# An adaLN transformer block on one core: batch one reordered, x reloaded into eight tiles, the last batch's norms moved by DMA

## The chip, the cores and the metric

The kernel runs on one core of one Trainium2 chip. The metric is the device time of one execution in microseconds (us). Engines are named as the profile names them: PE is TensorE (PEld its weight loads), DVE is VectorE, ACT is ScalarE, POOL is GpSimd, SP is SyncE. A name with a q behind it (SPq, ACTq, POOLq) is an engine's instruction queue, mostly where it issues DMAs.

## The reference

Four batches of 1024 tokens with 512 channels, all in float32. Six rows of modulation per batch come from a small vector c. Then an attention step and a linear FFN step, each with its layer norm, its shift and scale, and its gate:

```python
mod = (silu(c) @ wmod).reshape(B, 6, 1, 512)        # sa, ca, ga, sb, cb, gb
ga, gb = sign(ga) * max(|ga|, 0.25), sign(gb) * max(|gb|, 0.25)
h = layernorm(x) * (1 + ca) + sa
q, k = h @ Wq.T, h @ Wk.T                           # rank 64; every head has the same scores
attn = softmax(16 heads alike: sum over r of q_ir * k_jr)
x = x + ga * ((attn @ (h @ Wv.T)) @ Wo.T)
h = layernorm(x) * (1 + cb) + sb
x = x + gb * (sum over r of h @ factors[r] / sqrt(8) + bias)
```

## The kernel before

All 16 heads share one score matrix, so the attention is one 1024 x 1024 product per batch. Tokens are cut into eight tiles of 128 and two halves of four tiles. The matrices Wv and Wo are multiplied once into wvo, the eight factors are summed once into fsum, and the shift of the first norm goes through wvo into one row c1 per batch, which is added to x.

For each batch b the work is:

- ln1: statistics and normalized tiles xn (L309, L318), turned into hT. For batch zero PE transposes them (L331); for the others DVE transposes 32 x 32 blocks (L382) and 16 small DMAs, move_blocks (L371), put the blocks in place. A block is 64 KB. All of them are issued on SP unless another queue is named.
- project (L414), then scores for four pairs of token tiles (L460), each with a row maximum on DVE (nm, L476), an exponential on ACT (L480) and a transpose: by PE for pairs 0 and 1 of batch zero (L501), by DVE and move_blocks otherwise (L489, L371). Score tiles have two PSUM buffers, probability tiles two in SBUF.
- z: probabilities times xn for the two halves of query tokens. Batch zero does it plainly (z_steps, L527, two parts for each of four channel chunks); later batches use seven products of half size in place of eight (z_steps_by_seven, L595, steps m1, m5, m2, m6, m7, m3, m4), with sums on DVE and POOL around them.
- attn_out (o0 to o7, L665): z times w, where w is wvo scaled by ca and ga (make_w, L645); DVE adds the result into x (L670) and takes statistics. add_c1 (L362) adds the c1 row to x, bc_c being that row spread over all partitions by a DMA from DRAM.
- ln2: normalized tiles (L318) to hT_f. For batches zero to two DVE transposes blocks (L695), move_blocks brings them to a tile st (L371) and ACT applies shift and scale (L701). For the last batch PE transposes them (ln2_transposes, L331), woven between products. add_bias (L710) adds the bias row.
- ffn (f0 to f7, L725): hT_f times f, where f is fsum times the gate (make_f, L658); DVE adds x (L730) and a DMA stores the tile (L733).

PSUM products share four banks (ps_m). Batches are staggered: while batch b does its second half of z and attn_out, the projections and scores of batch b + 1 run between the steps; the FFN of batch b runs inside the first half of z of batch b + 1. The order is written out in the code, and a framework then places each engine's instructions and its waits. Each engine works its list in order.

The x tiles have twelve buffers: eight in use and four for the next batch (load_x, L101). For batches after the first, load_x goes to POOL's queue, as do the stores, so a load into a tile whose store is under way waits on that queue. xa tiles are a second read of x for ln1 of the next batch (load_xa, L112). The tiles st have one buffer; the spread rows (bc) have two. The factors are loaded and summed on POOL in batch zero (L285 to L293).

At the start the weights wv and wo come in four pieces each beside the x tiles of batch zero, all on SP. mod_products (L179) multiplies silu(c) with the modulation weights; for the rows sa and ca (name a) only two of the four column groups of PE are used, for the other four rows (name b) all four. mod_rows copies the PSUM rows to SBUF (L188), channels turns them by tiny PE transposes (L196), and qbias (L239) follows. shift_product (L251) makes c1 from sa and wvo.

Of the kernel before, what the change touches and what calls it, by code (L numbers as in the profile page):

```python
# [30 lines left out]
def kernel(  # L31
# [39 lines left out]
    stp = ctx.enter_context(tc.tile_pool(name="stp", bufs=1))  # L71
# [9 lines left out]
    def psum_mm(name):  # L81
        return ps_m.tile([P, 512], F32, tag="mm", name=name)
# [9 lines left out]
    nc.sync.dma_start(out=cTs, in_=cT.rearrange("(kc p) b -> p kc b", p=P))  # L92
# [5 lines left out]
    def load_x(b, t):  # L98
        tl = xp.tile([P, D], F32, tag="x", bufs=NT + GT, name=f"x_{b}_{t}")
        queue = nc.sync if b == 0 else nc.gpsimd  # L100
        queue.dma_start(out=tl, in_=x[b, ts(t, P), :])  # L101
        xt[b, t] = tl
        if b == 0:
            xa[b, t] = tl
# [16 lines left out]
    for cc in range(KC):  # L121
        nc.sync.dma_start(out=wvs[:, cc, :], in_=wv[ts(cc, P), :])
        nc.sync.dma_start(out=wos[:, cc, :], in_=woT[ts(cc, P), :])
        for t in range(2 * cc, 2 * cc + 2):
            load_x(0, t)
# [30 lines left out]
    scT = const.tile([P, KC, B], F32, name="scT")  # L156
    nc.vector.reciprocal(scT, en)
    nc.vector.tensor_tensor(scT, cTs, scT, ALU.mult)
# [26 lines left out]
    def mod_rows(ps, count, dst):  # L185
        rows = []
        for g in range(count):
            nc.vector.tensor_copy(dst[:, g, :], ps[32 * g : 32 * g + B, :])  # L188
            rows.append(dst[:, g, :])
        return rows  # L190
# [41 lines left out]
    def first_rows():  # L232
        sa_r, ca_r = mod_rows(mod_products([0, 1], "a"), 2, rows_a)
        first["sa"] = channels(sa_r, 0, "sa", 0.0)
        first["ca1"] = channels(ca_r, 0, "ca", 1.0)

        ps = psum_mm("ps_qbias")
        for kc in range(KC):
            nc.tensor.matmul(  # L239
                ps[: 2 * R, :B], wqk[:, kc, :], first["sa"][:, kc, :],  # L240
                start=(kc == 0), stop=(kc == KC - 1),
            )
        nc.vector.tensor_copy(qbias, ps[: 2 * R, :B])
# [3 lines left out]
    def shift_product():  # L247

        ps = psum_mm("ps_c1")
        for kc in range(KC):  # L250
            nc.tensor.matmul(  # L251
                ps[:B, :], first["sa"][:, kc, :], wvo[:, kc, :],
                start=(kc == 0), stop=(kc == KC - 1),
            )
        nc.vector.tensor_copy(rows_a[:, 2, :], ps[:B, :])
# [103 lines left out]
    def add_c1(b):  # L359
        bc = spread("c1", b)  # L360
        for t in range(NT):
            nc.vector.tensor_tensor(xt[b, t], xt[b, t], bc, ALU.add)  # L362

    def move_blocks(src, dst, queue=nc.sync):

        for r in range(NQ):
            for c in range(NQ):  # L370
                queue.dma_start(out=dst[ts(c, Q), r], in_=src[ts(r, Q), c])  # L371
# [307 lines left out]
    def ln2(b, g):  # L679


        if g == 0:
            bias_b[b] = spread("gbias", b)
        hT = hT2[b, g] = hp.tile([P, KC, GW], F32, tag="hT", name=f"hT_f_{b}_{g}")
        if b + 1 == B:
            xn = prp.tile([P, GT, D], F32, tag="pr", name=f"xn_f_{b}_{g}")
            xn2[b, g] = normalize(b, halves(g), mv2[b], xn, f"f_{b}_{g}")
        else:

            xn = hT.rearrange("p k w -> p (k w)")  # L690
            normalize(
                b, halves(g), mv2[b],
                xn.rearrange("p (c k t a) -> p t k c a", c=NQ, k=KC, t=GT), f"f_{b}_{g}",
            )
            nc.vector.transpose(xn, xn)  # L695
            st = stp.tile([P, NQ, KC * GT * Q], F32, tag="st", name=f"st_f_{b}_{g}")
            move_blocks(
                xn.rearrange("p (c n) -> p c n", c=NQ), st, nc.scalar if g == 0 else nc.sync
            )
            for kc in range(KC):  # L700
                nc.scalar.activation(  # L701
                    hT[:, kc, :].rearrange("p (t r a) -> p r t a", t=GT, r=NQ),
                    st[:, :, ts(kc, P)].rearrange("p r (t a) -> p r t a", t=GT),
                    AF.Identity, bias=second["sb"][:, kc, b : b + 1],
                    scale=second["cb1"][:, kc, b : b + 1],
                )
# [5 lines left out]
    def ln2_transposes(b, g):  # L712
        return [
            lambda kc=kc: transpose_group(
                xn2[b, g], hT2[b, g], kc, f"f_{b}_{g}",
                second["cb1"][:, :, b : b + 1], second["sb"][:, :, b : b + 1],
            )
            for kc in range(KC)
        ]

    def ffn(b, t):
        g, j = divmod(t, GT)
        ps = psum_mm(f"ps_f_{b}_{t}")
        for kc in range(KC):
            nc.tensor.matmul(  # L725
                ps, hT2[b, g][:, kc, ts(j, P)], fb[b][:, kc, :],
                start=(kc == 0), stop=(kc == KC - 1),
            )
        xi = xt[b, t]
        nc.vector.tensor_tensor(xi, ps, xi, ALU.add)  # L730

        queue = nc.sync if b + 1 == B else nc.gpsimd
        queue.dma_start(out=out[b, ts(t, P), :], in_=xi)  # L733
# [10 lines left out]
    wvo_chunk(3)  # L744
    for step in hT0[1][1]:
        step()
    first_rows()
# [8 lines left out]
    shift_product()  # L756
# [3 lines left out]
    hTn = []  # L760
    ln1(1, 0)
    hTn.append(hT_by_dma(1, 0))
# [3 lines left out]
    for b in range(B):  # L766
        nb = b + 1 if b + 1 < B else None
        if b == 0:
            z0 = z_steps(b, 0)
            z0[0]()  # L770
            softmax(0, 2)
            softmax(0, 3)
            ln1(1, 1)
            hTn.append(hT_by_dma(1, 1))
            gates()
            for step in z0[1:3]:
                step()
            add_c1(0)
            for step in z0[3:5]:
                step()  # L780
            scale_wqk(nb)
            for step in z0[5:]:
                step()
            second_channels()
            sum_factors()
        else:
            z0 = z_steps_by_seven(b, 0)
            for k, step in enumerate(z0):
                step()
                if k == 1:  # L790
                    make_f(b - 1)
                    for t in halves(0):
                        load_x(b, t)
                if k == 2 and nb is not None:
                    ln1(nb, 0)
                if k in (3, 4):
                    g = k - 3
                    add_bias(b - 1, g)
                    for t in halves(g):
                        ffn(b - 1, t)  # L800
                if k == 3:
                    for t in halves(1):
                        load_x(b, t)
                    if nb is not None:
                        hTn = [hT_by_dma(nb, 0)]
                        ln1(nb, 1)
                if k == 4 and nb is not None:
                    hTn.append(hT_by_dma(nb, 1))
                    scale_wqk(nb)
            p_sums(b, 1)  # L810
        z1 = z_steps(b, 1) if b == 0 else z_steps_by_seven(b, 1)
        after = {}
        if nb is not None:

            places = (0, 2, 3, 4, 5)
            todo = [lambda g=g: project(nb, g, hTn[g]) for g in range(2)]
            todo += [lambda p=p: softmax(nb, p) for p in range(len(places) - 2)]
            after = dict(zip(places, todo))
        for k, step in enumerate(z1):
            step()  # L820
            if k in after:
                after[k]()
            if k == 1:
                if b > 0:
                    add_c1(b)
                make_w(b)
        if nb is not None:
            n_sums(nb)
        for t in halves(0):
            attn_out(b, t)  # L830
            if t == 2 and nb is not None:
                scores(nb, 3)
        ln2(b, 0)
        if nb is not None:
            transpose_probs(nb, 3)
            for t in halves(1)[:2]:
                attn_out(b, t)
            p_sums(nb, 0)
            for t in halves(1)[2:]:
                attn_out(b, t)  # L840
        else:
            weave([lambda t=t: attn_out(b, t) for t in halves(1)], ln2_transposes(b, 0))
        ln2(b, 1)
    b = B - 1
    make_f(b)
    add_bias(b, 0)
    add_bias(b, 1)
    weave([lambda t=t: ffn(b, t) for t in halves(0)], ln2_transposes(b, 1))
    for t in halves(1):
        ffn(b, t)  # L850
# [33 lines left out]
```

## Time and profile before

| what | value |
|---|---|
| median of 3 runs | 561.77 us |
| lowest and highest | 559.41 and 562.37 us |
| the profiled execution, own time | 562.6 us |
| its span, first to last instruction | 559.8 us |
| PE busy | 534.8 us (96%), 1712 instructions |
| DVE busy | 359.3 us (64%) |
| POOL, ACT busy | 153.2 us (27%), 90.5 us (16%) |
| mean granted PE clock | 0.988 |
| DMA traffic | 71.97 MB, 37986 packets |

The profiled execution took 562.6 us, of which the span is 559.8; the rest lies before the first and after the last instruction. A matmul of 128 x 128 by 512 columns shows as two records, which start 0.43 us apart at full clock; their own durations (0.59 us) overlap. In the profile's lines the first number is the start or the busy time, names to the left of an arrow are written and to the right read, and brackets hold the engine's idle time before the instruction and what ended it.

### The profile page before, as it was taken

To read this page: it belongs to the slowest core of one execution; us is meant where nothing else is said; L and a number is where in the kernel's file an instruction comes from. 1 tells how busy PE (TensorE), PEld (TensorE's weight loads), DVE (VectorE), ACT (ScalarE), POOL (GpSimd) and SP (SyncE) were. 2 spreads that over 40 slices of the span, in tenths; PEclk is the share of its full clock that TensorE was granted. 3 is DMA by queue.
4 is the path that set the end of the run, shared out by engine and by line. 5 is a ranking of instruction groups with operands and counts; after the bars stand their busy time and mean duration, and the time that the engine had idled before them with its cause. 6 is when DMAs were issued, how large, how long until landed. Compare 5 with 4: busy or idle time off the path is not lost.

```text
span 559.8 us, 5238 instructions
## 1 busy us (share of the span) xinstructions
PE 534.8 (96%) x1712; PEld 293.9 (53%) x1712; DVE 359.3 (64%) x573; ACT 90.5 (16%) x150; POOL 153.2 (27%) x169
## 2 busy tenths in 40 slices
PE   6999899899999998999999998989999999999997
PEld 2443344343447554766448455756448458864442
DVE  4549991447499966638699786537899536336631
ACT  1314321013110220013112020121302010000000
POOL 2002313899900243253000333333000140010000
PEclk9989979899999999999999999999999999999999
DMA  8962546856445374622445536603443532000012
GB/s 305 381 235 75 150 111 195 244 168 221 126 100 136 102 234 144 191 64 58 103 103 131 166 104 178 203 10 76 103 117 100 150 124 83 0 1 0 0 75 76
DMA packets 37986, 71.97 MB, mean 129 GB/s; under 512 B 9460, under 2 KB 9972, under 8 KB 37960
## 3 DMA queue, kind: packets, MB, share of 16 engines
q1 hardware_dynamic: 27224, 40.41, 25.1%
q0 software_dynamic: 8432, 28.09, 15.8%
q10 hardware_dynamic: 2304, 3.15, 2.2%
q8 instruction: 13, 0.21, 0.2%
q14 instruction: 13, 0.11, 0.1%
HBM read 35.93 MB, written 8.42 MB: 79 GB/s over the span
## 4 chain that ended last, share of the span: by engine, by line
PE 50%; DVE 20%; issue 9%; SPq 9%; DMA 7%; POOL 3%; ACT 1%; POOLq 0%; DVEq 0%; ACTq 0%
PE ps_z_m L595 15%; PE ps_o L665 9%; PE ps_f L725 9%; SPq L371 8%; PE ps_qk L414 5%; PE ps_z L527 4%; PE ps_sc L460 3%; PE ps_wvo L166 3%; DMA out_dram<-x 2%; DMA hT_a<-st_a 2%; DVE nm L476 2%; DVE bn_f L309 1%; DVE hT_f L318 1%; DVE x L670 1%; DVE xn_a L318 1%
## 5 line engine op out<-in xcount | busy, mean ns | idle before, releaser
L725 PE MATMUL ps_f<-f,hT_f 128*128 128x512 f32 x256 | 112.3, 593 | 0.9 <-DVE x L730 0.8
L665 PE MATMUL ps_o<-w,zt 128*128 128x512 f32 x256 | 111.9, 593 | 0.0
L665 PEld LDWEIGHTS ps_o<-w,zt 128*128 128x128 f32 x256 | 48.1, 190 | 59.2 <-issue 56.8
L725 PEld LDWEIGHTS ps_f<-f,hT_f 128*128 128x128 f32 x256 | 48.1, 190 | 57.7 <-issue 51.7
L595 PE MATMUL ps_z_m<-pt,xn_a 128*128 128x256 f32 x288 | 65.3, 380 | 0.0
L527 PE MATMUL ps_z<-pt,xn_a 128*128 128x512 f32 x128 | 60.6, 628 | 3.0 <-DMA hT_a<-st_a 3.0
L595 PEld LDWEIGHTS ps_z_m<-pt,xn_a 128*128 128x128 f32 x288 | 54.6, 190 | 11.4 <-issue 2.2
L480 ACT ACTIVATE pr<-ps_sc,nm 128x1024 f32<-128x1024 f32 x32 | 35.6, 1113 | 92.0 <-DVE nm L476 48.4
L595 PE MATMUL ps_z_m<-pt,s 128*128 128x256 f32 x192 | 43.8, 381 | 3.7 <-DVE x L730 3.7
L304 POOL TENSOR_TENSOR r_f<-v_f,mhalf 128x4 f32<-128x4 f32 x8 | 9.3, 1163 | 131.9 <-DVE v_f L300 131.9
L527 PEld LDWEIGHTS ps_z<-pt,xn_a 128*128 128x128 f32 x128 | 25.2, 202 | 37.1 <-issue 36.3
L595 PEld LDWEIGHTS ps_z_m<-pt,s 128*128 128x128 f32 x192 | 36.1, 190 | 12.9 <-issue 8.3
L460 PE MATMUL ps_sc<-kT,qT 64*128 64x512 f32 x128 | 36.4, 636 | 2.7 <-ACT pr L480 2.7
L476 DVE TENSOR_REDUCE nm<-ps_sc 128x1 f32<-128x1024 f32 x32 | 37.6, 1206 | 0.5 <-PE ps_sc L460 0.5
L362 DVE TENSOR_TENSOR x<-x,bc_c 128x512 f32<-128x512 f32 x32 | 20.9, 686 | 25.4 <-DMA x<-in_x_dram 25.3
L670 DVE SCALAR_TENSOR_TENSOR x<-ps_o,ri,x 128x512 f32<-128x512 f32 x32 | 23.7, 742 | 19.6 <-PE ps_o L665 19.5
L730 DVE TENSOR_TENSOR x<-ps_f,x 128x512 f32<-128x512 f32 x32 | 21.3, 685 | 20.5 <-PE ps_f L725 20.5
L414 PE MATMUL ps_qk<-hT_a,wqk 128*128 128x512 f32 x64 | 30.6, 625 | 2.9 <-issue 1.6
L489 DVE STREAM_TRANSPOSE pr<-pr 128x2048 f32<-128x2048 f32 x14 | 32.2, 2299 | 1.1 <-DMA pt<-pr 0.9
L101 POOL DMA_DIRECT2D x<-in_x_dram x24 | 13.3, 556 | 64.1 <-DMA out_dram<-x 54.6
L293 POOL TENSOR_TENSOR fsum<-fsum,factor 128x512 f32<-128x512 f32 x24 | 30.4, 1273 | 0.7 <-DMA factor<-in_factors_dram 0.4
L428 DVE TENSOR_SCALAR qT<-ps_qk,qbias 64x512 f32<-64x512 f32 x8 | 5.9, 742 | 38.2 <-PE ps_qk L414 38.2
(125 smaller groups left out, 581.3 us busy)
## 6 DMA issues: line engine op xcount, KB each, us to landing
pt<-pr SPq DMA_DIRECT2D x224, 64.0 KB, 2.0
factor<-in_factors_dram POOLq DMA_DIRECT2D x16, 512.0 KB, 4.6
x<-in_x_dram POOLq DMA_DIRECT2D x24, 256.0 KB, 3.3
hT_a<-st_a SPq DMA_DIRECT2D x96, 64.0 KB, 3.0
out_dram<-x POOLq DMA_DIRECT2D x24, 256.0 KB, 3.3
xa<-in_x_dram POOLq DMA_DIRECT2D x20, 256.0 KB, 4.2
st_f<-hT_f ACTq DMA_DIRECT2D x48, 64.0 KB, 2.0
st_f<-hT_f SPq DMA_DIRECT2D x48, 64.0 KB, 2.0
```

The source lines that it names most:

```text
L293: nc.gpsimd.tensor_tensor(acc, acc, f[:, k], ALU.add)
L371: queue.dma_start(out=dst[ts(c, Q), r], in_=src[ts(r, Q), c])
L414: nc.tensor.matmul(ps[: 2 * R, :], wqkb[b][:, kc, :], hT[:, kc] if b == 0 else hT[:, :, kc], start=(kc == 0), stop=(kc == KC - 1),)
L460: nc.tensor.matmul(ps[:, ts(h, 512)], qT[h * R : (h + 1) * R, ts(i, P)], kT[h * R : (h + 1) * R, :], start=True, stop=True,)
L476: nc.vector.tensor_reduce(nm, ps, AX.X, ALU.max, negate=True)
L480: nc.scalar.activation(pr, ps, AF.Exp, bias=nm, scale=1.0, accum_out=den[:, k : k + 1])
L489: nc.vector.transpose(pr2, pr2)
L527: nc.tensor.matmul(hold[dc], xn1[b, jh][:, j - jh * GT, ts(dc, P)], PT[b, half][:, :, :, j, :], start=(j == 0), stop=(j == NT - 1),)
L595: nc.tensor.matmul(ps[:, ts(dc, 2 * P)], a[:, j, ts(dc, P)], m[:, :, j].rearrange("p r (k a) -> p k r a", k=2), start=(j == 0), stop=(j == ...
L665: nc.tensor.matmul(ps, ZT[b, half][:, kc, ts(j, P)], wb[b][:, kc, :], start=(kc == 0), stop=(kc == KC - 1),)
L670: nc.vector.scalar_tensor_tensor(xi, ps, rinv[b][:, t : t + 1], xi, ALU.mult, ALU.add)
L725: nc.tensor.matmul(ps, hT2[b, g][:, kc, ts(j, P)], fb[b][:, kc, :], start=(kc == 0), stop=(kc == KC - 1),)
```

## The change

It has four parts.

1. Start and batch zero. The first piece of wo and c are loaded from ACT's queue. The products for sa and ca are split over all four column groups of PE, two partial sums each (zero-padded to 32 columns); four products with a matrix sel add the partial sums and turn the rows into channels at once. c1's four products go to four column groups instead of one sum in PSUM, and ACT and DVE add the four rows. mod_rows is copied by ACT.
2. Order in batch zero. Pair 2's scores (the third pair) come before c1's product, pair 3's before ln1 of batch one, whose moves thus come after.
3. x reload and c1. x tiles have eight buffers instead of twelve, loads are pinned behind the stores (steps 5 and 6 of the first half of z), and the c1 adds are pinned to steps 3 to 6 of the second half of z. st gets two buffers.
4. Last batch. Its ln2 is moved by DMA like the others: first half on SP, second half on SP and ACT by turns; shift and scale on ACT and DVE by turns. attn_out of the first four tiles, the first ln2, make_f and the first add_bias come after m6, before m7, m3 and m4. The last FFN tile is computed and stored in two halves of 256 columns.

The diff, cut to its core:

```diff
-    stp = ctx.enter_context(tc.tile_pool(name="stp", bufs=1))
+    stp = ctx.enter_context(tc.tile_pool(name="stp", bufs=2))
...
-        tl = xp.tile([P, D], F32, tag="x", bufs=NT + GT, name=f"x_{b}_{t}")
+        tl = xp.tile([P, D], F32, tag="x", bufs=NT, name=f"x_{b}_{t}")
         queue = nc.sync if b == 0 else nc.gpsimd
-        queue.dma_start(out=tl, in_=x[b, ts(t, P), :])
+        load = queue.dma_start(out=tl, in_=x[b, ts(t, P), :])
+        if b > 0:
+            tc.keep_in_program_order(load)
...
-        nc.sync.dma_start(out=wos[:, cc, :], in_=woT[ts(cc, P), :])
+        (nc.scalar if cc == 0 else nc.sync).dma_start(out=wos[:, cc, :], in_=woT[ts(cc, P), :])
+        if cc == 0:
+            nc.scalar.dma_start(out=cTs, in_=cT.rearrange("(kc p) b -> p kc b", p=P))
...
     def mod_rows(ps, count, dst):
         for g in range(count):
-            nc.vector.tensor_copy(dst[:, g, :], ps[32 * g : 32 * g + B, :])
+            nc.scalar.copy(dst[:, g, :], ps[32 * g : 32 * g + B, :])
...
-    def first_rows():
-        sa_r, ca_r = mod_rows(mod_products([0, 1], "a"), 2, rows_a)
-        first["sa"] = channels(sa_r, 0, "sa", 0.0)
-        first["ca1"] = channels(ca_r, 0, "ca", 1.0)
+    def first_products():
+        ps = psum_mm("ps_mod_a")
+        for kk in range(KC // 2):
+            for m in range(2):
+                for kh in range(2):
+                    kc = 2 * kh + kk
+                    nc.tensor.matmul(
+                        ps[64 * m + 32 * kh : 64 * m + 32 * kh + 32, :], scT32[:, kc, :],
+                        wmods[m][:, kc, :], start=(kk == 0), stop=(kk == KC // 2 - 1),
+                    )
+        part = bcp.tile([P, D], F32, tag="bc", name="mod_a")
+        nc.vector.tensor_copy(part, ps)
+        return part
+    def first_channels(part):
+        ps = psum_mm("ps_ch_a")
+        for kc in range(KC):
+            nc.tensor.matmul(ps[:, ts(kc, 2 * B)], part[:, ts(kc, P)], sel, start=True, stop=True)
+        m = const.tile([P, KC, 2 * B], F32, name="mod_ch_a")
+        nc.vector.tensor_tensor(m, ps[...], plus, ALU.add)
+        first["sa"], first["ca1"] = m[:, :, :B], m[:, :, B:]
...
     def shift_product():
         for kc in range(KC):
             nc.tensor.matmul(
-                ps[:B, :], first["sa"][:, kc, :], wvo[:, kc, :], start=(kc == 0), stop=(kc == KC - 1),
+                ps[32 * kc : 32 * kc + B, :], first["sa"][:, kc, :], wvo[:, kc, :], start=True, stop=True,
             )
-        nc.vector.tensor_copy(rows_a[:, 2, :], ps[:B, :])
+    def shift_rows(ps):
+        nc.scalar.copy(c1, ps[:B, :])
+        for kc in range(1, KC):
+            nc.vector.tensor_tensor(c1, ps[32 * kc : 32 * kc + B, :], c1, ALU.add)
...
     def ln2(b, g):
-        if b + 1 == B:
-            xn = prp.tile([P, GT, D], F32, tag="pr", name=f"xn_f_{b}_{g}")
-            xn2[b, g] = normalize(b, halves(g), mv2[b], xn, f"f_{b}_{g}")
-        else:
...
+        queues = [nc.scalar if g == 0 else nc.sync]
+        if last:
+            queues = [nc.sync] if g == 0 else [nc.sync, nc.scalar]
+        move_blocks(xn.rearrange("p (c n) -> p c n", c=NQ), st, *queues)
...
+            if last and kc % 2:
+                nc.vector.tensor_scalar(dst, src, cb1, sb, ALU.mult, ALU.add)
+            else:
+                nc.scalar.activation(dst, src, AF.Identity, bias=sb, scale=cb1)
...
+        pieces = 2 if (b, t) == (B - 1, NT - 1) else 1      # in ffn
...
-    shift_product()
+    softmax(0, 2)
+    ps_c1 = shift_product()
...
-    hTn = []
-    ln1(1, 0)
-    hTn.append(hT_by_dma(1, 0))
...
             z0[0]()
-            softmax(0, 2)
             softmax(0, 3)
+            ln1(1, 0)
+            hTn = [hT_by_dma(1, 0)]
+            shift_rows(ps_c1)
+            for step in z0[1:3]:
+                step()
             ln1(1, 1)
...
-                    for t in halves(0):          # k == 1
-                        load_x(b, t)
...
-                if k == 3:
-                    for t in halves(1):
+                if k in (5, 6):
+                    for t in halves(k - 5):
                         load_x(b, t)
...
+            if nb is not None and k in (3, 4, 5, 6):
+                add_c1(b, (2 * k - 6, 2 * k - 5))
             if k == 1:
-                if b > 0:
-                    add_c1(b)
                 make_w(b)
+            if k == 3 and nb is None:
+                add_c1(b, halves(0))
+                for t in halves(0):
+                    attn_out(b, t)
+                ln2(b, 0)
+                add_c1(b, halves(1))
+                make_f(b)
+                add_bias(b, 0)
...
-            weave([lambda t=t: attn_out(b, t) for t in halves(1)], ln2_transposes(b, 0))
...
-    weave([lambda t=t: ffn(b, t) for t in halves(0)], ln2_transposes(b, 1))
-    for t in halves(1):
+    for t in range(NT):
         ffn(b, t)
```

## The prediction

> **What bounds the kernel now.** I read the page first, then the waits of PE, the busy time by stretch, the chain of waits, and last the timelines of the stretches where PE stood still.
>
> The page gives the bound:
>
> ```profile
> span 559.8 us, 5238 instructions
> ...
> PE 534.8 (96%) x1712; PEld 293.9 (53%) x1712; DVE 359.3 (64%) x573; ACT 90.5 (16%) x150; POOL 153.2 (27%) x169
> ...
> PEclk9989979899999999999999999999999999999999
> ```
>
> PE is busy all the time but 25.0 us, so the change can win only by removing products, by closing PE's gaps, or where the clock row dips. The waits of PE (total, times, longest) name the gaps:
>
> ```profile
> PE ps_wvo L166 <- DMA wos<-in_woT_dram: 5.3, 1, 5.3
> PE ps_z_m L595 <- DVE x L730: 3.7, 2, 2.1
> PE ps_z L527 <- DMA hT_a<-st_a: 3.0, 1, 3.0
> PE ps_sc L460 <- ACT pr L480: 2.7, 2, 1.9
> PE ps_qk L414 <- issue: 1.6, 1, 1.6
> PE ps_qk L414 <- DMA hT_a<-st_a: 0.9, 1, 0.9
> ```
>
> The busy time by stretch shows what follows the two gaps of batch one (PE busy; the granted clock is the third number from the end):
>
> ```profile
> 66.30:69.70 3.40, 1.30 (x5) 0.30 (x4) 3.27 (x5) 1.84 (x3) 0.10 (x1) 0.99 0.93 259
> 69.70:73.10 3.40, 2.77 (x5) 1.00 (x6) 3.37 (x4) 0.57 (x2) 1.13 (x3) 0.50 0.06 17
> 73.10:76.50 3.40, 3.40 (x5) 1.35 (x4) 3.40 (x5) 1.55 (x3) 0.48 (x1) 0.50 0.77 169
> 97.00:100.40 3.40, 0.55 (x8) 0.46 (x8) 2.88 (x4) 0.58 (x1) 3.00 (x4) 1.00 1.05 308
> 100.40:103.80 3.40, 3.21 (x4) 1.51 (x5) 2.52 (x3) 0.00 (x0) 1.21 (x2) 0.50 1.02 304
> ```
>
> A stretch of 3.4 us with 1.3 us or 0.55 us of work is followed by clock 0.50, so these gaps cost more than their idle time: 2.77/2 + 3.40/2 = 3.1 us after the first, 1.6 us after the second. A third spell at 0.51 (32.2 to 35.6) costs 1.7 us in the first projections.
>
> In batches one and two (counting from zero) the timeline of DVE shows why L595 waited:
>
> ```profile
> 210.06 0.69 DVE L362 TENSOR_TENSOR x<-x,bc_c 128x512 f32<-128x512 f32 x1 [2.93 <-DMA x<-in_x_dram]
> 210.67 0.68 DVE L730 TENSOR_TENSOR x<-ps_f,x 128x512 f32<-128x512 f32 x1
> 218.74 0.69 DVE L362 TENSOR_TENSOR x<-x,bc_c 128x512 f32<-128x512 f32 x1 [3.65 <-DMA x<-in_x_dram]
> 219.35 2.48 DVE L730 TENSOR_TENSOR x<-ps_f,x 128x512 f32<-128x512 f32 x4
> ```
>
> and that of POOL where the x tile was:
>
> ```profile
> 211.20 0.55 POOL L101 DMA_DIRECT2D x<-in_x_dram  x1 [4.55 <-DMA out_dram<-x]
> ```
>
> Stores and loads alternate on POOL's queue, each load waiting about 4 us for the store of the tile it replaces. DVE sits at the c1 add of that tile, the FFN evictions (L730) queue behind it, and PE runs out of PSUM.
>
> **The change, part by part.** Times are of this execution (span 559.8 us, its own time 562.6, the shown median 561.8).
>
> *Start to first projection.* Only wos moves beside wvs; it is issued at about 1.24 instead of 1.78, so PE starts 0.5 us earlier (4.75). The matmul chunks up to 24.14 are then bound by PE. mod_a is 16 records of 0.43 us half-hidden pairwise: 3.44 us. In four column groups it needs 4 rounds of 0.43 = 1.7 us if all four run together, as mod_b's records do at 44.7 (four starts within 0.02 us); transposes are put between them, so I take 2.2. The two row copies (1.4 us, PE idle 1.2 us behind them) and eight tiny transposes (0.8) become one copy of 0.69 us under the transposes of hT, four small products (1.0, as L239's eight records) and one add (0.2). Sum: chunks end 21.9, mod_a and 16 transposes (1.75) 25.9, channels 26.9, add 27.1, qbias 28.15. First projection at 28.2 instead of 31.16: **-3.0**. Four x tiles no longer load at 11.9 on POOL's queue (1 MB in a stretch that moves 385 GB/s), so wm_a comes earlier, not later. The memsets and sel's two adds stand on idle POOL and DVE before 9 us: nothing.
>
> *To the second half of z.* Before: 31.16 to 100.59, 69.4 us. After, by steps from 28.2: project 6.9, scores and mod_b up to 45.6 as before (but for the spell), then 12 transposes, scores of pair 2, c1. c1 drops from eight records (3.44) to two rounds (0.86): 2.6 us of work gone. What is late next is the path DVE to ACT to PSUM: nm of pair 2 stands behind ln1(1,0)'s statistics (2.8), its normalizations (1.9) and two transposes (1.25), and so runs at about 51.1 to 52.3; exp to 53.7; then ACT copies c1 and a probability block, which frees the bank for the last transpose at 54.85. PE waits there about 2.5 us, and 0.3 us twice more. Then scores and z_0 run without a wait: 55.3 + 0.95 + 0.3 + 3.45 + 2.85 + 3.44 + 20.6 + 0.5 = 87.5. The moves that the second half needs are now ahead of most of hT(1,0) on SP: pair 3's transpose ends near 68.9, its 16 issues of 0.637 us (10.2) at 79.1, landed 80.6, against need at 87.5. So 59.3 us: **-10.1**. The rest of hT(1,0) lands near 87.8 (needed 94.4) and hT(1,1) near 98 (needed 105.7): moved past 32 issues on SP, at no cost, with 7 us in hand. The mod rows and the first c1 row move to ACT (five copies, by its 128x512 copies 0.59 each), counted in that path already. The clock: two new low spots remain (25.9 to 28.2, and the 2.5 us wait). Each may cost a spell of 1.7 or nothing; I take half: **+1.7**. The spell at 100.4 goes: **-1.6**.
>
> *Middle of batches one and two.* Loads go to the end of all stores, adds to the score rounds, and two st buffers end DVE's wait for the hT move (5.0 us at 227.4). Gaps of PE: 0.75 + 1.64 + 0.15 + 0.91 and 0.13 + 2.07 + 1.56: **-7.2**. Cover of the reload: eight issues of 0.55, the last behind the store of tile 7 (about 5 us after the last FFN product), landed by 10 us; the first add stands some 31 us behind that product. Behind the loads on POOL stand the sums of the next batch's norms, first used by its second z product, some 60 us later. What is late next is nothing on PE: hT(2,0) and hT(2,1) would land near 338 and 348 on the old clock, needed at 351 and 358.
>
> *The c1 adds.* 8 x 0.61 = 4.9 us on DVE in the score rounds of three batches. DVE idles 2.69 + 0.41 + 0.85 behind the third round (266 to 277), so it gets about 1 us later; the FFN's input has 3.1 us in hand (first activation done 306.3, product at 309.48). In batch zero POOL's sums of factors run beside them, where w took 1.26 us an operation against 0.68 later. Bounds 0 and 2; I take **+0.5**, nearer to the row with cover.
>
> *Tail.* Let A be the end of m6 (484.54 before). Gone: 32 transposes (8 x 0.43 = 3.4) and waits and fill of 2.3; before, PE ends at A + 71.4. Pure work is 10.4 + 55.2. New path: o3 ends A + 13.8; eviction, statistics, POOL's power (1.03), four normalizations and one bias add to 19.3, transpose 2.3, 16 issues on SP. These rows give what a move costs:
>
> ```profile
> 293.86 10.17 ACTq L371 DMA_DIRECT2D st_f<-hT_f  x16
> ...
> 305.57 2.94 ACT L701 ACTIVATE hT_f<-st_f,mod_sb,mod_cb 128x512 f32<-128x512 f32 x4 [0.37 <-DMA st_f<-hT_f]
> ```
>
> So st(3,0) lands at about A + 33.3. In DVE's order two activations of that tile stand ahead of the c1 adds of tiles 4 to 7, and so ahead of o4's eviction: DVE waits from 26.7 to 33.3. Adds to 37; the last frees the buffer of bc_gb, whose load takes 3.9 us (release 467.05, used 471.00), so f starts at 41, between statistics. PE, done with o7 at 38.8, waits 2.8. Evictions, f and statistics end at 46, power 47, normalizations and bias 49.5, transpose 51.9, eight issues on each of SP and ACT 57.3, landed 58.8, first activation 59.6. PE ends its first four FFN tiles at 55.4, waits 4.2, works 13.8: 73.4, and with a clock spell of 1.7 at even odds 74.2. The last tile in two halves saves 0.3 of eviction and perhaps 0.3 of store. **+2.2**, bounds -6.6 (nothing waits) and +5.
>
> A rule speaks against these small moves. The Trainium skill, DMA: Bandwidth & Descriptors, section Bandwidth, puts 64 KB at 0.95 us of transfer and wants far larger ones; one after another, 16 would take 15.2 us by it, an estimate. The row shows 10.17 for 16, so issue is the price and they overlap; by the rule the tail would be some 5 us longer, near 549 in all. In this trace 1.95 and 0.78 us of idle, with 1.1 us of work between, were followed by clock 0.50, which is why I count a spell at even odds for a 2.5 us wait. The skill's TensorE: Matmul & The Clock Gate, section HAM oscillation, warns only of gaps above about 3.4 us; by it that wait would cost no spell, 0.85 less.
>
> Sum: -3.0 - 10.1 + 1.7 - 1.6 - 7.2 + 0.5 + 2.2 = -17.5. On the median: 561.8 - 17.5 = 544.3.
>
> **Rivals.** *The tail hides.* If the framework's waits are looser than I read them, the moves lie under products: tail -6.6, total 535.5. For: m7, m3, m4 and four output tiles give 24 us of cover. Against: DVE's order. 0.12.
>
> *Batch one's waits only move.* Work removed stays removed (3.0 + 2.6), but waits and spells return behind the DVE-ACT path: -3.0 - 2.6 - 7.2 + 0.5 + 2.2 = -10.1, 551.7. For: DVE is 9.1 to 9.8 of 10 us busy from 40 to 80. 0.14.
>
> *The reload doesn't free DVE* (store waits still reach an add): 7.2 stays, 551.5. 0.05.
>
> *Slower: DVE sets the score rounds.* A round takes DVE 6.49 (nm at 250.98 and 257.47), PE 5.57; with 1.22 of adds 7.71. If two score buffers tie PE to it, 3 x 2.14 + 2.4 = 8.8 a batch, 26.5 in three: 561.8 - 17.5 + 26.5 = 571. It decides from the point where DVE's lateness passes the 3.1 us in hand. Against: the 3.95 us of idle behind the rounds. 0.07.
>
> **How the numbers follow.** Forecast 544.3 with chance 0.60, and 0.02 for sums that cancel. The range 535 to 553 holds it with its bounds, the first three rivals, and leaves out the slower one and the ends. About 0.5%, 2.8 us, is what a measurement can tell from no change: faster 0.90, same 0.03, slower 0.07.
>
> **What would show it.** Right: no PE wait on DMA hT_a at z or on L730's successor; first projection near 28, second half of z near 88; PE gaps near 54 and twice in the last 35 us. Wrong: clock below 1.00 after 110 other than in the tail, or idle PE at the score rounds.

## The result and the profile after

The changed kernel takes 565.1 us, the kernel before 562.2 us beside it: ratio 1.0087, 95% interval 1.0059 to 1.0116. It is slower by a little under 1% where 544.3 us (535 to 553) was forecast. The profiled execution of after took 562.9 us, its span is 561.1 us (before: 562.6 and 559.8), so the spans can be set against each other. Line numbers in the rows are those of each version's own kernel; in after L410 is the c1 add, L527 the row maximum, L531 the exponential, L338 a sum of factors, and L616 to L619 are POOL's sums of the next batch's norms.

The page of after:

```profile
span 561.1 us, 5229 instructions
...
PE 528.7 (94%) x1688; PEld 293.0 (52%) x1688; DVE 373.7 (67%) x574; ACT 93.2 (17%) x155; POOL 154.3 (28%) x171
```

PE has 6.1 us less to do than before (528.7 against 534.8) and yet the span is 1.3 us longer; DVE is busy 14.4 us longer for one instruction more. The waits of PE (total, times, longest):

```profile
PE ps_sc L511 <- ACT pr L531: 6.8, 4, 4.9
PE ps_z_m L646 <- DVE pt L658: 6.6, 1, 6.6
PE ps_wvo L184 <- DMA wos<-in_woT_dram: 5.9, 1, 5.9
PE ps_f L770 <- ACT hT_f L756: 4.1, 1, 4.1
PE ps_pt L552 <- ACT pt L557: 2.1, 2, 1.4
PE ps_f L770 <- DVE f L709: 1.7, 1, 1.7
PE ps_o L716 <- DVE zt L684: 1.7, 1, 1.7
```

The old waits are gone: none on hT_a, none on an FFN eviction. The first line has grown (2.7 before, at another place) and the second is new; both end on DVE (pr is ScalarE's exponential, which waits for DVE's maxima). Cut at five instructions of PE that both kernels have, the spans compare so (us, from the timelines of PE):

| stage of PE | before | after | difference | forecast |
|---|---|---|---|---|
| start to first projection | 31.16 | 30.32 | -0.84 | -3.0 |
| to the second half of z, batch zero | 69.43 | 58.39 | -11.04 | -10.1 + 1.7 |
| to batch zero's first FFN product | 85.85 | 103.08 | +17.23 | -1.6 and a part of +0.5 |
| to the product behind batch two's FFN | 277.07 | 270.22 | -6.85 | -7.2 and a part of +0.5 |
| to the end of the span | 96.29 | 99.09 | +2.80 | +2.2 |

Four of five stages went the forecast's way. The third ate all of it. DVE's timeline there:

```profile
119.35 2.31 DVE L540 STREAM_TRANSPOSE pr<-pr 128x2048 f32<-128x2048 f32 x1 [0.21 <-issue]
121.58 5.47 DVE L410 TENSOR_TENSOR x<-x,bc_c 128x512 f32<-128x512 f32 x2
126.98 2.34 DVE L527 TENSOR_REDUCE nm<-ps_sc 128x1 f32<-128x1024 f32 x2
...
133.65 13.23 DVE L410 TENSOR_TENSOR x<-x,bc_c 128x512 f32<-128x512 f32 x2
146.81 2.34 DVE L527 TENSOR_REDUCE nm<-ps_sc 128x1 f32<-128x1024 f32 x2
...
153.04 2.45 DVE L410 TENSOR_TENSOR x<-x,bc_c 128x512 f32<-128x512 f32 x4
```

Eight c1 adds (L410) take 5.47 + 13.23 + 2.45 = 21.15 us, where the eight took 4.88 before. One add of the second pair lasted 12.63 us by itself:

```profile
133.65 12.63 DVE L410 TENSOR_TENSOR x<-x,bc_c 128x512 f32<-128x512 f32 x1
```

The row of before:

```profile
81.07 4.88 DVE L362 TENSOR_TENSOR x<-x,bc_c 128x512 f32<-128x512 f32 x8
```

POOL's timeline beside the slow pair:

```profile
131.58 2.36 POOL L616 TENSOR_TENSOR s<-xn_a,xn_a 128x1024 f32<-128x1024 f32 x1
133.90 1.25 POOL L338 TENSOR_TENSOR fsum<-fsum,factor 128x512 f32<-128x512 f32 x1
...
142.17 2.33 POOL L619 TENSOR_TENSOR s<-xn_a,s 128x1024 f32<-128x1024 f32 x1
144.47 1.25 POOL L338 TENSOR_TENSOR fsum<-fsum,factor 128x512 f32<-128x512 f32 x1
```

The add that began at 133.65 ended at 146.3, its own 0.6 us behind the end of POOL's row of sums (144.47 + 1.25 = 145.7). The four adds after that row take 0.61 each. Behind each slow pair stand the maxima of the next scores (L527), so the exponentials and the next scores come late (PE waits 4.87 and 0.80), and DVE, with hardly a pause until 187, is still late when L658 is due, the sum that the fourth z product of batch one reads (PE waits 6.57).

### The profile page after: what moved, and what is told of

It reads as the page before. It is cut to its first block, busy times and chain, and to the rows that moved or that the text cites. A ratio compares the mean times of both kernels' runs of the same rounds, so it can differ in the third digit from the quotient of the medians.

```text
span 561.1 us, 5229 instructions
## 1 busy us (share of the span) xinstructions
PE 528.7 (94%) x1688; PEld 293.0 (52%) x1688; DVE 373.7 (67%) x574; ACT 93.2 (17%) x155; POOL 154.3 (28%) x171
## 4 chain that ended last, share of the span: by engine, by line
PE 44%; DVE 15%; SPq 6%; issue 3%; DMA 1%; POOL 1%; ACT 1%; POOLq 0%; DVEq 0%; ACTq 0%
PE ps_z_m L646 17%; PE ps_f L770 16%; PE ps_o L716 7%; SPq L422 6%; PE ps_qk L465 2%; DVE pr L540 2%; DVE hT_f L363 2%; DVE hT_f L743 2%; DVE x L721 1%; DVE bn_f L354 1%; POOL r_f L349 1%; ACT pr L531 1%; DVE x L760 1%; DVE nm L527 1%; DMA pt<-pr 1%
## 5 line engine op out<-in xcount | busy, mean ns | idle before, releaser
L770 PE MATMUL ps_f<-f,hT_f 128*128 128x512 f32 (+1 forms) x264 | 113.1, 586 | 5.9 <-ACT hT_f L756 4.1
L770 PEld LDWEIGHTS ps_f<-f,hT_f 128*128 128x128 f32 x264 | 50.5, 193 | 65.4 <-issue 57.6
L578 PE MATMUL ps_z<-pt,xn_a 128*128 128x512 f32 x128 | 56.9, 597 | 0.0
L775 DVE TENSOR_TENSOR x<-ps_f,x 128x512 f32<-128x512 f32 (+1 forms) x33 | 21.9, 669 | 47.7 <-PE ps_f L770 47.7
L646 PE MATMUL ps_z_m<-pt,s 128*128 128x256 f32 x192 | 45.8, 394 | 6.6 <-DVE pt L658 6.6
L531 ACT ACTIVATE pr<-ps_sc,nm 128x1024 f32<-128x1024 f32 x32 | 35.5, 1112 | 92.8 <-DVE nm L527 46.1
L511 PE MATMUL ps_sc<-kT,qT 64*128 64x512 f32 x128 | 39.6, 650 | 6.8 <-ACT pr L531 6.8
L527 DVE TENSOR_REDUCE nm<-ps_sc 128x1 f32<-128x1024 f32 x32 | 37.6, 1209 | 2.5 <-PE ps_sc L511 2.4
L756 ACT ACTIVATE hT_f<-st_f,mod_sb,mod_cb 128x512 f32<-128x512 f32 x28 | 20.6, 803 | 102.6 <-DMA st_f<-hT_f 75.9
L410 DVE TENSOR_TENSOR x<-x,bc_c 128x512 f32<-128x512 f32 x32 | 36.2, 1179 | 0.0
L349 POOL TENSOR_TENSOR r_a<-v_a,mhalf 128x4 f32<-128x4 f32 x8 | 9.2, 1150 | 80.4 <-DVE v_a L345 80.1
L338 POOL TENSOR_TENSOR fsum<-fsum,factor 128x512 f32<-128x512 f32 x24 | 30.6, 1281 | 0.6 <-DMA factor<-in_factors_dram 0.2
L778 POOL DMA_DIRECT2D out_dram<-x x24 | 13.2, 549 | 58.4 <-DVE x L775 48.2
```

Of the source, the lines that this page charges most:

```text
L338: nc.gpsimd.tensor_tensor(acc, acc, f[:, k], ALU.add)
L349: nc.gpsimd.tensor_tensor(r, v, mhalf[:, :n], ALU.pow)
L410: add = nc.vector.tensor_tensor(xt[b, t], xt[b, t], bc_c1[b], ALU.add)
L511: nc.tensor.matmul(ps[:, ts(h, 512)], qT[h * R : (h + 1) * R, ts(i, P)], kT[h * R : (h + 1) * R, :], start=True, stop=True,)
L527: nc.vector.tensor_reduce(nm, ps, AX.X, ALU.max, negate=True)
L531: nc.scalar.activation(pr, ps, AF.Exp, bias=nm, scale=1.0, accum_out=den[:, k : k + 1])
```

## The experiments

Each timed version ran beside the kernel before on the same chip.

| version | us | before beside it | ratio, 95% interval |
|---|---|---|---|
| adds early | 551.0 | 561.3 | 0.983, 0.979 to 0.987 |
| adds early, decoys late | 553.3 | 562.5 | 0.987, 0.982 to 0.991 |
| before, adds late | 573.0 | 561.3 | 1.021, 1.016 to 1.026 |
| few sums | 560.0 | 561.3 | 0.998, 0.995 to 1.001 |
| tail reordered | 558.7 | 563.2 | 0.993, 0.989 to 0.997 |
| adds early, old tail | 551.9 | 563.2 | 0.982, 0.974 to 0.989 |
| adds early, tail reordered, start | 544.1 | 563.2 | 0.970, 0.962 to 0.977 |
| the same, wqk scaled on ScalarE | 542.5 | 562.5 | 0.966, 0.962 to 0.970 |

**Adds early.** One part undone, for batch zero alone:

```
             gates()
+            add_c1(0, range(NT))
...
-            if nb is not None and k in (3, 4, 5, 6):
+            if nb is not None and b > 0 and k in (3, 4, 5, 6):
```

> The changed kernel with the eight c1 adds of batch zero alone put back ahead of GpSimd's sums of factors (after the gates); those of the other batches stay late. Theory A (beside GpSimd's back-to-back sums an add of two SBUF tiles stands until the sums pause: eight adds took 21.15 us in the changed kernel instead of 8 x 0.61 = 4.9): the adds take 4.9 to 6 us, PE's waits of 4.87, 0.80 and 6.57 us and the clock dips with them go, the time falls by about 16 us to 549 (546 to 552). Rival B (the adds are late work on a full VectorE, by their number and place in its order, and slow durations are not the cause): only their 4.9 us moves, 559 to 561. Rival C (the waits come from the transfers of the probabilities or of the norms, moved past each other on SyncE's queue): 564 to 566, waits stay.

Measured 551.0. DVE's timeline and PE's waits:

```profile
87.19 4.91 DVE L410 TENSOR_TENSOR x<-x,bc_c 128x512 f32<-128x512 f32 x8 [5.08 <-DMA bc_c<-rows_c]
```

```profile
PE ps_f L770 <- ACT hT_f L756: 4.1, 1, 4.1
PE ps_sc L511 <- ACT pr L531: 3.1, 3, 2.0
```

Eight adds, 4.91 us; the wait on L658 is gone and that for scores is more than halved. A, not B or C, though the new place also takes the adds out of DVE's crowded stretch; the next run separates these.

**Decoys.** The early adds stay, and eight reads of one tile take the late adds' places in DVE's order:

```
+            if b == 0 and k in (3, 4, 5, 6):
+                for t in (2 * k - 6, 2 * k - 5):
+                    idle = small.tile([P, 6], F32, tag="bn", name=f"idle_{t}")
+                    tc.keep_in_program_order(nc.vector.bn_stats(idle, xt[b, t]))
```

> A control for the load: the version with the early adds (551.0 in its comparison) plus eight operations that read one tile alone (batch-norm statistics of the x tiles, 0.6 to 0.7 us each, results unused), pinned in VectorE's order exactly where the late adds stood. If the late adds cost because of their number and place (4.9 us on a full VectorE), the loss returns: 560 to 566, PE waits for scores over 4 us. If only because they read two SBUF tiles beside GpSimd's sums: each statistic takes 0.7 us, 551 to 553.5.

Measured 553.3, within the second expectation. DVE's timeline, in the place of the pair that took 13.23:

```profile
131.79 1.24 DVE L870 BATCH_NORM_STATS2 idle<-x 128x6 f32<-128x512 f32 x2
```

So the number and the place of the late operations cost at most about 2 us (553.3 against 551.0, and the two intervals overlap). What costs the rest is their kind: an add of two SBUF tiles beside POOL's sums, where the decoy reads one tile and writes six columns. Which kinds are slow is measured below.

**Before, adds late.** The reverse: in the kernel before, batch zero's adds alone are put, pinned, into the places they have in the change.

```
-            add_c1(0)
...
+            if b == 0 and k in (3, 4, 5, 6):
+                add_c1(b, (2 * k - 6, 2 * k - 5))
```

> The kernel before with one thing alone: batch zero's eight c1 adds pinned late, two behind each of the steps 3 to 6 of its second half of z, as in the change. Theory A: the adds meet GpSimd's sums, which run back to back from about 139 to 153 us, single adds take over 5 us, PE waits for scores; slower by 8 to 16 us, 570 to 578. Rival B: VectorE has 5.9 us of idle there for 4.9 us of adds, within 2 us of before, 561 to 564. Rival C: no effect, 562.

Measured 573.0. The one moved part makes the kernel before 2.1% slower. Of the pair in this row one add took 14.76 us:

```profile
137.28 15.36 DVE L365 TENSOR_TENSOR x<-x,bc_c 128x512 f32<-128x512 f32 x2
```

**Few sums.** In sum_factors:

```
-                else:
-                    for k in range(2):
-                        nc.gpsimd.tensor_tensor(acc, acc, f[:, k], ALU.add)
+                elif r == 2:
+                    nc.gpsimd.tensor_tensor(acc, acc, f[:, 0], ALU.add)
```

> The changed kernel with 20 of the 28 GpSimd operations that sum the factors left out (two of seven for each row of 128; all loads stay), so the sum of factors is not the reference's; the c1 adds stay late. Theory A: without sums beside them the late adds take 0.6 to 0.7 us each, batch zero's PE waits of 4.87 and 6.57 go to under 1 us each, about 549 (545 to 552). Rival B (load and order of VectorE): adds stay where they are and the waits with them, 562 to 566. Rival C: 562 to 566.

Measured 560.0: a miss for A in size. With POOL free sooner, the sums of the next batch's norms (L615 to L618 in this version) began at 122.69 instead of 131.58 and stood beside the first pair of adds:

```profile
127.44 6.10 DVE L409 TENSOR_TENSOR x<-x,bc_c 128x512 f32<-128x512 f32 x2
140.15 1.25 DVE L409 TENSOR_TENSOR x<-x,bc_c 128x512 f32<-128x512 f32 x2
```

The pair beside those sums took 6.10 us, the pair behind them 1.25, and all eight 9.80. PE still waited 5.5 us for scores behind that pair. The loads of the factors came in a shorter time as well, and PE had a new wait of 2.1 us on hT_a. The edit moved more than it took away, so its total says little; its two rows agree with A.

**The cost by itself.** Kernels of stages. ScalarE copies make both engines end a stage before either begins the next; the core is

```
for k in range(10):
    nc.gpsimd.tensor_tensor(y, d, y, ALU.subtract)
for k in range(4):
    nc.vector.tensor_tensor(a, c, a, ALU.subtract)    # or another operation
```

First, four DVE operations alone and beside ten of POOL that depend on each other.

> Not the reference's computation: twelve stages, in each four VectorE operations on 128x512 tiles, alone or beside ten GpSimd tensor-tensor operations (1.25 us each) that run back to back, or with a load issued on GpSimd's queue after every second or every one of them. Theory A: two SBUF inputs alone 0.6 to 0.7 us; beside back-to-back sums the first of the four lasts until the sums end (about 12 us), then 0.6 to 0.7; with a load after every second 2.5 to 4 us each, after every one 1.5 to 2.5. One SBUF input, PSUM with SBUF, and the 32x32 transposes: as alone. If instead each operation is passed in turn, an add would take at most 2 us in every stage; if bandwidth is shared, all four would be slowed alike.

```profile
6.78 2.87 DVE L66 TENSOR_TENSOR a<-c,a 128x512 f32<-128x512 f32 x4 [2.65 <-ACT a L56]
10.19 5.70 DVE L66 TENSOR_TENSOR a<-c,a 128x512 f32<-128x512 f32 x4 [0.53 <-ACT a L56]
...
79.83 2.05 DVE L72 TENSOR_SCALAR a<-a,col 128x512 f32<-128x512 f32 x4 [9.64 <-ACT a L56]
82.42 4.69 DVE L72 TENSOR_SCALAR a<-a,col 128x512 f32<-128x512 f32 x4 [0.54 <-ACT a L56]
...
100.14 2.87 DVE L75 TENSOR_TENSOR a<-ps,a 128x512 f32<-128x512 f32 x4 [0.53 <-ACT a L56]
...
117.54 2.95 DVE L78 STREAM_TRANSPOSE a<-a 128x512 f32<-128x512 f32 x4 [0.54 <-ACT a L56]
```

Of the first two pairs the upper row is DVE alone. Adds of two SBUF tiles double, as does the scaling of one SBUF tile, which had been expected to be free; the add of PSUM and SBUF (2.87 alone) and the transposes (2.95 alone) are as alone. But the adds took turns with POOL's operations, 1.6 us each; none lasted to the end. Nor did they with a load issued after every second or after every one of POOL's operations (5.96 and 5.95 us for four). By that eight adds would cost about 8 us more and not 16. Four more kernels looked for what makes the long one.

Dependence between POOL's operations:

> Not the reference's computation: eleven stages, in each four VectorE operations on 128x512 tiles beside ten GpSimd ones. The former stages had every GpSimd operation take the result of the one before, and adds took turns with them (1.63 us each); in the changed kernel, where operations on different tiles follow each other (start to start 1.22 us, with no gap), one add lasted 12.63 us. Theory A1 (an engine keeps the way to SBUF as long as its next operation needn't wait for its last): beside a chain of dependent operations 1.6 us an add; beside operations that alternate between two tiles, the first add lasts until they end, 10 to 12.5 us, and with a load issued after every second of them about 2.5 us, after every one 1.6 us. Theory A2 (turns are always taken): 1.6 us an add in every stage, and the 12.63 us has another cause. The scaling of one SBUF tile (0.51 us alone) as the adds.

A1 fell: 1.6 to 1.8 us an add whether POOL's operations depend on each other or not. One add in the stage with a load issued on POOL's queue after every second operation lasted 6.80 us; with a load after every one the four took 5.95, in turns. When POOL starts, against the adds:

> Not the reference's computation: ten stages of four VectorE adds beside ten GpSimd operations on two tiles in turn, GpSimd's start put off against the adds' by a ScalarE copy of growing width (about 0.2 to 0.8 us in all). The adds that lasted 4.45, 6.80, 12.63 and 14.76 us had begun 0.07 to 0.25 us ahead of a GpSimd operation. If that decides, some offsets give an add of 10 us or more and the others turns of 1.6 to 1.8 us; if not, turns in all ten.

Turns in all ten (longest add 1.75 us). When the adds arrive:

> Not the reference's computation: thirty-two stages in which ten GpSimd operations run first and two VectorE adds arrive behind 32x32 transposes of growing length (steps of 64 columns, about 0.07 us), so that they arrive at every point of a GpSimd operation. In sixteen stages GpSimd alternates two 128x512 tiles, in sixteen it alternates a 128x1024 and a 128x512 tile, as in batch zero. If the point of arrival decides between one turn and many, a few stages show an add of 8 us or more (it lasts until the ten have ended) and the rest an add of 0.6 to 3 us; the mixture alone may do it, as in batch zero; if no stage does, the long adds have a cause that these stages leave out.

No add over 2.42 us in 32 stages: neither the point of arrival nor the mixture of sizes. Last, loads issued on POOL's queue:

> Not the reference's computation: four groups of eight stages, each with ten GpSimd operations and four VectorE adds behind transposes of eight lengths. Group one: three loads issued on GpSimd's queue first, then the operations on two tiles in turn; two: a load after every second; three: after every third; four: three loads first, then 128x1024 operations on three different tiles in turn with 128x512 ones. If loads issued on that queue bring the long adds, groups one to three hold some adds of over 4 us, as the 6.80 us before; if it is operations with three different tiles, only group four; if neither, all adds end within 2.5 us and the cause stays open.

Of group one, the second add of a first stage, and the first two of the stage behind it:

```profile
9.71 1.74 DVE L138 TENSOR_TENSOR a<-c,a 128x512 f32<-128x512 f32 x1
...
23.85 12.52 DVE L137 TENSOR_TENSOR a<-c,a 128x512 f32<-128x512 f32 x1
36.29 0.68 DVE L138 TENSOR_TENSOR a<-c,a 128x512 f32<-128x512 f32 x1
```

In every second stage of group one the first add lasted until POOL's ten operations had ended (12.52, 12.25, 11.78, 11.50 us). With a load after every second or third operation many adds lasted 3.1 or 4.3 us, about the length of POOL's run between two loads; in group four 4.04. So an add lost one turn to a POOL that only computed, and could lose all of them to one that had issued loads. In the changed kernel POOL issues the loads of the factors among its sums, the last at 129.61, and then computes to 145.7 without a pause. The trace of the stages shows a pause as one difference: in the four with a long add POOL's operations followed its loads at once, in the other four POOL stood idle for 2.0 to 2.8 us between them (the copies that part the stages hold back its operations, not its loads). A pause alone doesn't decide: in group four the operations followed the loads at once too, and no add lasted over 4.04. So why some stages and not all stays open; that moving those loads to another queue would save the late adds was not tried, since SyncE and ScalarE carry the moves and exponentials of the same stretch.

**The tail.** Only the order of the last batch is altered:

```
-                add_c1(b, halves(0))
+                add_c1(b, range(NT))
+                make_f(b)
                 for t in halves(0):
                     attn_out(b, t)
                 ln2(b, 0)
-                add_c1(b, halves(1))
-                make_f(b)
-                add_bias(b, 0)          # now behind the z products
...
-            if last and kc % 2:
+            if last and g == 1 and kc % 2:
```

> The changed kernel with only the order of the last batch's work altered: all eight c1 adds and f ahead of its attention outputs, the first half's four scalings of the transposed norms all on ScalarE, bias adds behind the z products. By the trace of the changed kernel the three waits of PE in the tail (1.7 on VectorE's sums of z, 1.7 on f, 4.1 on the second half's norms) come from VectorE standing from 510.3 to 516.3 us at a scaling that waits for its transfer: 1.7 + 1.7 + about 3.5 go, 558 (555 to 561). If instead the transfers themselves set the time (24 and 8 issues), only the 1.7 for f goes: 563.

Measured 558.7. From the product behind batch two's FFN to its last product PE takes 88.8 us (after: 95.9, before: 92.5). The waits on zt and f are gone and that on hT_f is down:

```profile
PE ps_f L770 <- ACT hT_f L756: 2.2, 1, 2.2
```

The waits on f and hT_f go back to this one row of DVE's timeline in the changed kernel; behind it stood four c1 adds, the eviction of the fifth attention tile and f:

```profile
516.26 1.00 DVE L754 TENSOR_SCALAR hT_f<-st_f,mod_cb,mod_sb 128x512 f32<-128x512 f32 x2 [5.95 <-DMA st_f<-hT_f]
```

The wait on zt has another cause than the expectation says: it was over at 510.36, as DVE's pause began. DVE had put four bias adds ahead of the last sums of z and then stood twice for POOL's (1.44 and 0.65 us); in this version's code those bias adds stand behind the z products.

**Old tail.** Early adds, with TensorE's transposes and the order of before for the last batch (the minus lines of the diff for ln2, ln2_transposes and the two weaves put back), and its c1 adds together:

```
-            if k == 3 and nb is None:
-                add_c1(b, halves(0))
...
+            if k == 1 and nb is None:
+                add_c1(b, range(NT))
```

> The version with the early adds (551.0 in its own comparison) with the last batch's norms transposed by TensorE again and its operations in the order of before; only the last tile's two halves are kept. By the traces the tail after the last wait-free product took 75.1 us in the changed kernel and 71.4 before: 551 - 3.5 = 547.5 (545 to 549). If the transfers cost nothing over the transposes, 551; if products removed from PE are worth more than the waits, 553.

Measured 551.9, no gain. The version made a wait of its own: its c1 adds stand early, and now meet the late reload of x.

```profile
PE ps_z_m L646 <- DVE t L629: 3.2, 1, 3.2
```

Without these 3.2 us its last stretch of PE is 92.4 us, as before (92.5), against 96.1 with the new tail of the early-adds version. So 3.7 us of tail are there in the stretch, and the new wait takes them back; whether the total would show them otherwise was not run.

**All three.** Early adds, the reordered tail, and

```
-        (nc.scalar if cc == 0 else nc.sync).dma_start(
+        nc.sync.dma_start(
             out=wos[:, cc, :], in_=woT[ts(cc, P), :]
```

> Adds early, the altered order of the tail, and the first block of wos issued on SyncE's queue again beside wvs: 551 - 7 for the tail's waits - 0.6 for the start = 543.4 (540 to 547). If VectorE's order is not what makes the tail wait: 550.

Measured 544.1, as the sum had it. PE starts at 4.7 us. This beats both kernels. That it lands on the 544.3 forecast for the changed kernel is chance: its last stretch of PE takes 89.0 us against 92.5 before, where the forecast had the tail 2.2 longer than before.

**wqk on ScalarE.** The same, and in scale_wqk:

```
+            if b == 2:
+                nc.scalar.mul(w[:, kc, :], wqk[:, kc, :], first["ca1"][:, kc, b : b + 1])
...
```

> The version with all three (adds early, order of the tail, start; 544.1) and the four scalings of wqk for batch two, which took VectorE 5.24 us beside the sums and 0.86 without them, moved to ScalarE. Theory A: the PE waits for scores of batch one (2.3 us in all) and the clock dip behind them go, 541 (539.5 to 543). If they are cover for something else: 544.

Measured 542.5 (ratio 0.966 against 0.970, intervals that overlap: no difference shown). There was less to win than the expectation says: in the version that it builds on the four scalings took 2.92 us, not 5.24. The waits for scores stayed at 2.3 us, because ScalarE ran three of the scalings ahead of its evictions of q and k, and the scores came later:

```profile
116.59 2.36 DVE L530 TENSOR_REDUCE nm<-ps_sc 128x1 f32<-128x1024 f32 x2 [2.88 <-PE ps_sc L514]
```

The wait changed its engine.

## Why the prediction was wrong, step by step

**The step that failed** is the term "The c1 adds": +0.5, bounds 0 and 2. The text had the sign in hand ("In batch zero POOL's sums of factors run beside them, where w took 1.26 us an operation against 0.68 later") and then took the value "nearer to the row with cover". Measured: 16.3 us of DVE time (21.15 - 4.88), and +17.2 us in PE's stage. Early adds alone take back 13 to 14 us (565.1 beside a before of 562.2, 551.0 beside one of 561.3). The trace of before could have priced it better from two rows. Four scalings of 128x128 took 4.97 us beside the sums, where one elsewhere took 0.28, and w took up to 3.73 us for two:

```profile
97.87 3.73 DVE L645 SCALAR_TENSOR_TENSOR w<-wvo,mod_ca,bc_ga 128x512 f32<-128x512 f32 x2
...
120.28 4.97 DVE L398 TENSOR_SCALAR wqk<-wqk,mod_ca 128x128 f32<-128x128 f32 x4
```

By the row of w, 1.87 an operation, eight adds are 10 us longer, which was a bound to keep, and with DVE's 5.9 us of idle in that stretch a loss for PE. The rival on the slower side ("DVE sets the score rounds") had the right engine and rounds and a wrong price: it took 0.61 for the add, and so spread 8.8 us over each of three batches. Batches one and two, where POOL doesn't sum at that time, show nothing of it: 1.25 to 1.28 us for each pair of late adds.

The Trainium skill, SBUF — State Buffer, section "SBUF: two separate sides", says that VectorE and GpSimd share a pair of ports as an exclusive lock. A VectorE operation takes it in a two-port mode, or with two SBUF inputs against a GpSimd operation that reads SBUF; whichever engine starts first has the pair for its whole instruction, and the other stands. The stages agree for two SBUF tiles (slowed) and for PSUM with SBUF and the transposes (not slowed). The scaling of one SBUF tile was slowed as well; that it runs in a two-port mode no run here shows. On how long, the measurements differ from the page: at most one GpSimd instruction for each add (up to 2.4 us) in every stage without loads, but up to 12.5 us, ten instructions, in some stages with loads, and 14.8 us for one add of the version of before with late adds.

**The rest of that stage.** Of +17.2 us, PE's waits are 4.87 + 0.80 + 6.57 = 12.2. The scores of batch one's first pair are now in two parts of four records that take 1.98 us each, where eight took 1.99 before: +1.9, not forecast. The gain of 1.6 for the old clock spell is real; of the balance of 4.7, 3.7 is lower clock behind the two long waits (eight scores in 3.43 us instead of 1.99, sixteen products in 5.83 instead of 3.62; the granted clock was 0.57 from 129.4 to 132.9 us and 0.50 from 186.1 to 189.5), and 1 is not accounted for.

**Start**, forecast -3.0, got -0.84. PE began at 5.92 instead of 4.75: the first block of wos, from ScalarE's queue, came later than from SyncE's (PE began at 4.7 and 4.5 in the two versions that issue it there, at 5.2 to 5.5 in the five others with the changed start). mod_a took 2.96 us and not 2.2.

**To the second half of z**, forecast -8.4 (the terms of its one long sum add up to 87.4, not 87.5), got -11.04. The two waits on ScalarE's copies came where said, 0.60 and 1.45 against 2.5 and twice 0.3, and without the clock spells counted at 1.7.

**Middle**, forecast -7.2, got -6.85: the reload works as read, and no PE wait on an FFN eviction is left.

**Tail**, forecast +2.2, got +2.80. The first moved tile was used 33.5 us after A (482.73; forecast 33.3); f came at A + 40.8 (41), the last wait was 4.10 (4.2) with its clock spell in full (FFN tiles in 15.49 us instead of 13.9). Not forecast was o4's wait of 1.7 behind bias adds and POOL's sums of z; with PE later by that, f's wait was 1.73 and not 2.8. That the total came near is in part luck. It was DVE's order, not the moves, that cost: reordered, the same moves beat the transposes by 3.7 us (92.5 - 88.8).

## What to carry to other kernels

Before an operation is moved into an idle slot of its engine, look at what GpSimd does in that slot: an add of two SBUF tiles on VectorE, or the scaling of one, has no fixed duration beside GpSimd's arithmetic, and the duration from a quiet stretch is then no price. Price it from the slowest row of that kind in the same stretch, and where the stretch feeds the bound engine, put the operation ahead of the sums (the early adds) or let one of its inputs come from PSUM (as alone in the stages; not tried in the kernel). In a tail, the wait of an engine in order is charged to whatever stands behind it: one scaling that waits for a transfer held four adds, an eviction and a weight.

## What had not been expected of the hardware

Loads issued on GpSimd's queue can change how long an add on VectorE lasts: 0.7 us alone, 1.6 to 2.4 beside sums without loads, up to 12.5 in some stages with them. The scaling of one SBUF tile with a column is slowed too (2.05 us for four alone, 4.69 beside the sums). And PE's clock differs from run to run at the same place: the 16 records of the first projection took 7.11 us in after and 8.81 in the version with early adds, behind the same 0.28 us of idle (granted clock 1.00 against 0.80 over that stretch), so a spell there is not to be forecast from one trace.
